# Retention layer: sums of absolute values shared between quads by adds on GpSimd, and normed images in the shared ring

## The chip, the cores and the metric

The kernel runs on one core of a Trainium2 chip. Its time is the device time of one launch in microseconds (us), the median of several runs. The core has five engines that work from queues of their own, each in order: TensorE (PE in the profile; its weight loads are PEld), VectorE (DVE), ScalarE (ACT), GpSimd (POOL) and SyncE (SP), which issues most of the transfers. Engines wait for one another through semaphores. Matrix products are written to a small memory of their own, PSUM, which VectorE and ScalarE read and GpSimd does not in this kernel.

## The reference

Four layers are applied one after the other to 8 images of 32 x 32 tokens with 256 channels, each as `x = x + layer(group_norm(x))`. The change touches the first layer alone, a retention layer with 8 heads of 32 channels. Cut to what matters:

```python
q, k, v = xf @ Wq.T, xf @ Wk.T * 32 ** -0.5, xf @ Wv.T     # per head: 1024 tokens x 32
qr, kr = theta_shift(q, sin, cos), theta_shift(k, sin, cos)  # x*cos + rotated(x)*sin
qk = einsum('bhqd,bhkd->bhqk', qr, kr) * mask                # 1024 x 1024 per head
den = clip(abs(qk).sum(-1), 1.0, 50000.0)
out = einsum('bhqk,bhkd->bhqd', qk / den, vr)
out = (out - mean) / sqrt(var + 1e-5) * ln_g + ln_b          # over the 32 channels of a head
out = gelu(out) @ Wo.T
```

So each score is needed twice: itself in the product with the values, and its absolute value in the sum `den` over the keys.

## The kernel before

The host hands the image over with channels in the partitions. A *quad* is the unit of the layer: `quads[n] = (b, c, h, kb)` is image `b`, four of the eight heads (`c`), half of the queries (`h`, 512 of them) and a block of 128 keys (`kb`). There are 32 quads to an image and 256 in all; what is called a position below is a quad's number within its image, 0 to 31. For quad `n` the program has

- `scores(n)`: for each of two pairs of heads (`i`) two matmuls of 32 channels into a tile `s` of two PSUM banks, and one product on VectorE (L681) with the mask, which gives `e[n, i]`, 128 keys x two heads x 512 queries;
- `absolute(n, i)`: ScalarE's absolute value `ea[n, i]` of that (L685), in a ring of four buffers;
- `sums(n)`: four matmuls with a column of ones (L693), one head each, side by side in the four groups of columns of the array, which add up `ea` over the keys in the PSUM tile `sm`; the eight quads of one `(b, c, h)` accumulate, and after the last VectorE clamps the sum to `dn` (L701);
- `nums(n)`: four matmuls with the values, also side by side (L720), which accumulate in `num`; after the eighth ScalarE copies it to `nm` (L728).

The loop in the last lines of `layer0` emits for each `n` scores and first absolute value, sums of quad `n - 2`, products with the values of quad `n - 1`, the second absolute value, and then `fill.emit(n)`: the units of other work that `fill.add(at, unit)` put down for this quad, ordered by `at`. Units that take matmuls are the projections `project` (each half of the queries or keys of four heads, then a shuffle on VectorE, a copy on ScalarE and the rotation on GpSimd, L560 to L567), the values `values`, the variance `var` and the output `output`. They take the place of a pair in the ring of three two-bank PSUM tiles that the scores use (`pair`, three buffers). `tail` prepares the norm over a head's channels: Square of `dn` on ScalarE, square of `nm` on GpSimd (L578) and their sum (L579), and then mean by matmul, logarithm and exponential, the product on VectorE (L591) and Gelu.

For the next image, group statistics (`gn.stats`, `gn.mean`, `gn.root`) and `normed(b + 1)` (two GpSimd operations, L236) are spread as units too. The normed image `xn` has one buffer of its own, and the images `x` share a ring of three buffers (`K.big`) with first tiles of the next layer; an image is loaded two images ahead, at position 16.

The order of TensorE, VectorE and ScalarE is the order in which the program is written (`manual_schedule`); the order on GpSimd and SyncE is set by the scheduler. Every engine works its queue in order, so a unit that waits holds up all that is written after it on its engine.

Of the kernel before, what the change touches and what calls it, by code (L numbers as in the profile page):

```python
# [436 lines left out]

class Fillers:
# [22 lines left out]
def layer0(tc, K, src, dst, n_img, a, first):  # L461
    nc = tc.nc
    with tc.tile_pool(name="l0c", bufs=1) as cp, tc.tile_pool(
# [51 lines left out]
        xn, v, qk, hT, nm, dn, turned = ({} for _ in range(7))  # L515
# [5 lines left out]
        def normed(b):  # L521
            gn.shift(b)
            xn[b] = wk.tile([P, 2, L], F32, name="xn")
            for c in range(2):
                gn.apply(nc.gpsimd, b, c, xn[b][:, c, :], x[b][:, c, :])
# [16 lines left out]
        def project(b, s, c, h):  # L542
# [13 lines left out]
            if h == 0:  # L556
                return
            d = wk.tile([P, L], F32, name=f"qk{s}{c}")
            qk[b, s, c] = d
            nc.gpsimd.tensor_mul(v3(sh), v3(sh), hankel(63))  # L560
            nc.gpsimd.tensor_mul(v3(xc), v3(xc), hankel(0))
            if s == 1:
                nc.gpsimd.tensor_add(d, xc, sh)
            else:
                nc.gpsimd.tensor_add(xc, xc, sh)
                o = 126 + 32 * c
                nc.gpsimd.tensor_mul(  # L567
                    v3(d), v3(xc), rot[:, o : o + 32].unsqueeze(2).to_broadcast([P, 32, 32])
                )


        def tail(b, c):
            m, d = nm.pop((b, c)), dn.pop((b, c))
            if c == 0:
                hT[b] = wk.tile([P, 2, L], F32, name="hT")
            nc.scalar.activation(d, d, AF.Square, scale=math.sqrt(1e-5))
            sq = wk.tile([P, L], F32, name="sq")
            nc.gpsimd.tensor_mul(sq, flat(m), flat(m))  # L578
            nc.gpsimd.tensor_add(sq, sq, flat(d))  # L579
# [17 lines left out]
            return var, norm  # L597
# [16 lines left out]
        def prepare(b):  # L614

            n = 32 * b
            for i in range(4):
                fill.add(
                    n + (0, 1, 3, 4)[i],
                    lambda s=1 - i // 2, h=i % 2: project(b, s, 1, h),  # L620
                )
            if b == 0 and n_img > 1:
                x[1] = load(1)
                measure(1, 6)
            if b + 2 < n_img:
                def ahead():
                    x[b + 2] = load(b + 2)

                fill.add(n + 16, ahead)
                measure(b + 2, n + 23)  # L630
            if b + 1 < n_img:
                fill.add(n + 15, lambda: normed(b + 1))
                for i in range(4):
                    fill.add(
                        n + (17, 18, 20, 21)[i],
                        lambda s=1 - i // 2, h=i % 2: project(b + 1, s, 0, h),
                    )
                    fill.add(n + 23 + i, lambda u=i: values(b + 1, u))

        def measure(b, at):  # L640
            for i in range(4):
                fill.add(at + i, lambda i=i: gn.stats(b, image_parts(x[b]), i))
            fill.add(at + 5, lambda: gn.mean(b))
            fill.add(at + 7, lambda: gn.root(b))

        def follow(nx):
            n = 32 * n_img
            for i, u in enumerate(nx.early()):
                fill.add(2 + i if i else 0, u)
            fill.add(n - 46, nx.load)  # L650
            for i in range(4):
                fill.add(n - 38 + i, lambda i=i: nx.stats(i))
            fill.add(n - 33, nx.mean)
            fill.add(n - 31, nx.root)
            for c in range(2):
                fill.add(n - 27 + c, lambda c=c: nx.norm(c))
            fill.add(n - 12, nx.weights)
# [9 lines left out]

        def scores(n):
            b, c, h, kb = quads[n]
            o = (28 - 4 * kb) * 32 + HALF * h  # L670
            for i in range(2):
# [11 lines left out]
        def absolute(n, i):  # L683
            ea[n, i] = wk.tile([P, 2, HALF], F32, name="ea", bufs=4)
            nc.scalar.activation(ea[n, i], e[n, i], AF.Abs)  # L685

        def sums(n):
            b, c, h, kb = quads[n]
            if kb == 0:
                acc["sm"] = pp.tile([P, HALF], F32, tag="sm", name="sm")  # L690
            for j in range(4):
                g = slice(32 * j, 32 * j + 32)
                nc.tensor.matmul(  # L693
                    acc["sm"][g, :], ones, ea[n, j // 2][:, j % 2, :],
                    start=kb == 0, stop=kb == 7,
                )
            del ea[n, 0], ea[n, 1]
            if kb == 7:
# [5 lines left out]
                if h == 1:  # L704
                    var, norm = tail(b, c)
                    fill.add(n + 7, var)
                    for h in range(2):
                        fill.add(n + 9 + h, lambda h=h: norm(h))
                    if c == 1:
                        for i in range(4):  # L710
                            fill.add(n + 12 + i, lambda i=i: output(b, i // 2, i % 2))

        def nums(n):
# [11 lines left out]
            if kb == 7:  # L725
                if h == 0:
                    nm[b, c] = wk.tile([P, 2, HALF], F32, name="nm", bufs=2)
                nc.scalar.copy(nm[b, c][:, h], acc["num"])  # L728

        engines = {mybir.EngineType.PE, mybir.EngineType.DVE, mybir.EngineType.Activation}  # L730
        with tc.manual_schedule(engines=engines):
# [3 lines left out]
            normed(0)  # L735
            for s in (1, 0):
                for h in range(2):
                    project(0, s, 0, h)
            for u in range(4):
# [4 lines left out]
            for n in range(N + 2):  # L744
# [5 lines left out]
                if n >= 2:  # L750
                    sums(n - 2)
# [1611 lines left out]
```

## Time and profile before

| what | value |
|---|---|
| median of 3 runs | 3330.99 us (3329.07 to 3332.86) |
| the profiled execution's own time | 3334.75 us |
| its span | 3333.0 us |
| busy in the span: TensorE, VectorE, ScalarE, GpSimd | 96%, 66%, 68%, 45% |
| mean granted clock of TensorE | 0.976 |
| first layer | about 0 to 1090 us of the span |
| period of one image within it (issue of output to issue of output) | 130.36 us |

A line of the timeline or of a group reads: engine, line of the kernel, operation, tile written <- tiles read, and shapes; `x8` counts instructions, and a float32 matmul is two of them. Idle time before an instruction is followed by `<-` and what ended it. Position of a quad and the loop's `n` are not in the profile; they are counted from the groups of scores (L675).

### The profile page before, as it was taken

Reading aid. Unit: us, or ns where it says so; the run is one execution under the profiler, and the core shown is the slowest. Engines: PE = TensorE matmul, PEld = TensorE weight load, DVE = VectorE, ACT = ScalarE, POOL = GpSimd, SP = SyncE. Lnnn points to the kernel's source line nnn. Section 1 sums busy time; section 2 is a strip of 40 time slices with the busy share of each in tenths; the row PEclk is TensorE's granted clock in tenths of the full one; section 3 lists DMA queues with packets and bytes.
Section 4 is the critical chain, followed back from the end, with each engine's and each line's share of the span. In section 5 each row is a group of like instructions: output and inputs, shape, how many; then the busy total and the mean of one; then the engine's idle time right before and its main releaser. Section 6 shows DMA issues by size and latency. Waiting matters only on the chain. (4 is left out here: it accounts for less than half of the span.)

```text
span 3333.0 us, 77642 instructions
## 1 busy us (share of the span) xinstructions
PE 3203.6 (96%) x30792; PEld 1649.6 (49%) x30792; DVE 2185.0 (66%) x5570; ACT 2277.6 (68%) x5066; POOL 1491.7 (45%) x1073
## 2 busy tenths in 40 slices
PE   7999999999998999899999999999998999999997
PEld 3323323233232444667677766666664555555554
DVE  4776776777676667565555655666665667777775
ACT  3666666666676457755556547767676779888885
POOL 4233223323431011245444445344335658888777
PEclk9999999999999999999999999999998889999999
DMA  3000000000000666777787731111111001101001
GB/s 141 14 26 1 26 26 1 26 7 20 26 1 32 221 235 238 234 202 191 193 216 200 187 115 58 53 65 40 50 52 36 14 14 38 35 30 36 27 27 61
DMA packets 139183, 268.00 MB, mean 80 GB/s; under 512 B 9218, under 2 KB 77700, under 8 KB 130500
## 3 DMA queue, kind: packets, MB, share of 16 engines
q1 hardware_dynamic: 132436, 242.67, 24.3%
q10 hardware_dynamic: 6384, 20.37, 1.8%
q8 instruction: 243, 3.98, 0.5%
q14 instruction: 120, 0.98, 0.1%
HBM read 177.81 MB, written 85.20 MB: 79 GB/s over the span
## 5 line engine op out<-in xcount | busy, mean ns | idle before, releaser
L681 DVE TENSOR_TENSOR e<-s,ret 128x1024 f32<-128x1024 f32 x512 | 602.9, 1219 | 180.4 <-PE s L675 176.4
L685 ACT ACTIVATE ea<-e 128x1024 f32<-128x1024 f32 x512 | 535.1, 1055 | 267.8 <-DVE e L681 233.9
L675 PE MATMUL s<-qk,qk 32*128 32x512 f32 x2048 | 300.4, 640 | 2.4 <-POOL qk L567 1.7
L1564 POOL TENSOR_TENSOR e<-e,su 128x616 f32<-128x616 f32 (+2 forms) x128 | 157.3, 1229 | 269.8 <-DVE su L1563 240.2
L693 PE MATMUL sm<-ea,ones 128*32 128x512 f32 x2048 | 273.0, 604 | 2.0 <-DVE dn L701 2.0
L720 PE MATMUL num<-e,v 128*32 128x512 f32 x2048 | 266.6, 592 | 0.0
L1711 DVE COPY pts<-pt 112x512 f32<-112x512 f32 x256 | 175.9, 687 | 133.4 <-PE pt L1706 131.7
L2076 ACT ACTIVATE e<-win,disc 128x196 f32<-128x196 f32 x512 | 239.7, 544 | 0.3
L843 PE MATMUL up_ps<-x,wup 128*128 128x512 f32 x512 | 230.7, 605 | 3.2 <-POOL x L236 3.2
L1696 POOL TENSOR_TENSOR e<-e,su 128x784 f32<-128x784 f32 x128 | 191.3, 1495 | 82.7 <-DVE su L1695 53.9
L1688 ACT ACTIVATE e<-e,mx 128x196 f32<-128x196 f32 x512 | 228.0, 454 | 0.0
L2083 POOL TENSOR_TENSOR e<-e,win 128x784 f32<-128x784 f32 x128 | 201.7, 1576 | 37.8 <-issue 31.6
L1559 ACT ACTIVATE e<-e,mx 128x154 f32<-128x154 f32 (+2 forms) x512 | 212.3, 426 | 0.0
L1059 ACT ACTIVATE d<-d,cols 128x128 f32<-128x128 f32 x512 | 163.8, 392 | 67.9 <-POOL d L1050 67.8
L870 DVE SCALAR_TENSOR_TENSOR cv<-xm,par,cv 128x512 f32<-128x512 f32 x192 | 144.7, 754 | 85.5 <-ACT cv L865 80.9
L2015 PE MATMUL qkv_ps<-xq,w 128*128 128x512 f32 x384 | 191.4, 625 | 1.2 <-ACT fac L2110 1.2
L1255 POOL TENSOR_TENSOR decayed<-state,rb 128x520 f32<-128x520 f32 x48 | 50.8, 1058 | 304.7 <-PE sc L1188 112.5
L1796 PE MATMUL qkv_ps<-x,w 128*128 128x512 f32 x384 | 182.7, 613 | 1.6 <-POOL x L236 1.6
L1706 PEld LDWEIGHTS pt<-idg,e 128*112 128x112 f32 x1024 | 120.3, 139 | 120.5 <-issue 90.6
L675 PEld LDWEIGHTS s<-qk,qk 32*128 32x128 f32 x2048 | 85.3, 183 | 184.2 <-issue 120.4
L1706 PE MATMUL pt<-idg,e 128*112 128x128 f32 x1024 | 164.7, 287 | 8.4 <-DVE oT L1730 3.1
L1678 DVE CUSTOM_DVE_ANT_0 e<-s,e 128x196 f32<-128x196 f32 x512 | 153.7, 357 | 8.0 <-PE s L1665 4.2
(244 smaller groups left out, 6775.6 us busy)
## 6 DMA issues: line engine op xcount, KB each, us to landing
d<-l1rows SPq DMA_DIRECT2D x64, 512.0 KB
x<-x SPq DMA_DIRECT2D x25, 1024.0 KB
l1xm<-xm SPq DMA_DIRECT2D x16, 1024.0 KB
l1sz<-sz SPq DMA_DIRECT2D x16, 1024.0 KB
xv<-l1xm SPq DMA_DIRECT2D x32, 512.0 KB
l1xa<-xa SPq DMA_DIRECT2D x16, 1024.0 KB
xa<-l1xa SPq DMA_DIRECT2D x16, 1024.0 KB
rb<-l1rows SPq DMA_DIRECT2D x32, 512.0 KB
```

The costliest lines, as they stand in the source:

```text
L675: nc.tensor.matmul(s[:, j % 2], qk[b, 1, c][g, kb * P : (kb + 1) * P], qk[b, 0, c][g, h * HALF : (h + 1) * HALF], start=True, stop=True,)
L681: nc.vector.tensor_mul(e[n, i], s, m)
L685: nc.scalar.activation(ea[n, i], e[n, i], AF.Abs)
L693: nc.tensor.matmul(acc["sm"][g, :], ones, ea[n, j // 2][:, j % 2, :], start=kb == 0, stop=kb == 7,)
L720: nc.tensor.matmul(acc["num"][g, :], v[b][:, kb, vc], e[n, j // 2][:, j % 2, :], start=kb == 0, stop=kb == 7,)
L843: nc.tensor.matmul(ps, wup[:, kc, m * P : (m + 1) * P], seg(s)[:, kc], start=kc == 0, stop=kc == 1,)
L1559: self.nc.scalar.activation(p[:, j], p[:, j], AF.Exp, scale=-1.0, bias=mx[:, j : j + 1], accum_out=su[:, j : j + 1],)
L1688: self.nc.scalar.activation(e[:, j], e[:, j], AF.Exp, scale=-1.0, bias=mx[:, j : j + 1], accum_out=self.su[:, j : j + 1],)
L1706: self.nc.tensor.transpose(ps[: self.PART, at : at + P], self.tile(n)[:, 2 * i + j, k * self.PART : (k + 1) * self.PART], self.K.ident,)
L2015: nc.tensor.matmul(ps, w[:, kc, o : o + P], xq[b][:, kc, h * HALF : (h + 1) * HALF], start=kc == 0, stop=kc == 1,)
L2076: nc.scalar.activation(e[:, j], win[:, 0], AF.Tanh, scale=disc[b][:, i, 8 + h : 9 + h], bias=disc[b][:, i, h : h + 1],)
L2083: nc.gpsimd.tensor_add(e, e, win[:, 1].unsqueeze(1).to_broadcast([P, 4, NWIN]))
```

## The change

Absolute values of two consecutive quads are added before they are summed, for two of the four heads in turn. In quads 0 and 1 of each group of four the order of the head pairs is `(0, 1)`, in quads 2 and 3 it is `(1, 0)`; on every odd quad GpSimd adds the quad before to the first pair in place. Four quads then have six tiles `ea` instead of eight, and three sets of sums take them, at the fourth quad of the group and at the first and second of the next; the third quad of a group has no sums. The ring of `ea` has six buffers.

With it go: GpSimd's order is now the written one too; the rotation is split in units of one operation (`rotate`), one per quad; the square of `nm` becomes a unit of its own (`squared`), and Square and sum become the unit `total`; the normed image comes from the shared ring (`K.big`), so that an image is loaded one image ahead at position 9, has its statistics at 12 and 13, mean and root at 15 and 16 and its two norm operations at 18 and 19; positions of projections and values move; and `follow` places the first pieces of the next layer accordingly.

```diff
-        def normed(b):
-            gn.shift(b)
-            xn[b] = wk.tile([P, 2, L], F32, name="xn")
-            for c in range(2):
-                gn.apply(nc.gpsimd, b, c, xn[b][:, c, :], x[b][:, c, :])
+        def normed(b, c):
+            if c == 0:
+                gn.shift(b)
+                xn[b] = K.big("xn")
+            gn.apply(nc.gpsimd, b, c, xn[b][:, c, :], x[b][:, c, :])
...
+        def rotate(b, s, c, i):
+
+            sh, xc = turned[0], turned[1]
+            if i == 0:
+                qk[b, s, c] = wk.tile([P, L], F32, name=f"qk{s}{c}")
+                nc.gpsimd.tensor_mul(v3(sh), v3(sh), hankel(63))
+            elif i == 1:
+                nc.gpsimd.tensor_mul(v3(xc), v3(xc), hankel(0))
+            elif i == 2:
+                nc.gpsimd.tensor_add(qk[b, s, c] if s else xc, xc, sh)
+            else:
+                o = 126 + 32 * c
+                nc.gpsimd.tensor_mul(
+                    v3(qk[b, s, c]), v3(xc),
+                    rot[:, o : o + 32].unsqueeze(2).to_broadcast([P, 32, 32]),
+                )
+
+        def squared(b, c):
+            sqs[b, c] = wk.tile([P, L], F32, name="sq")
+            m = flat(nm[b, c])
+            nc.gpsimd.tensor_mul(sqs[b, c], m, m)
...
-            nc.scalar.activation(d, d, AF.Square, scale=math.sqrt(1e-5))
-            sq = wk.tile([P, L], F32, name="sq")
-            nc.gpsimd.tensor_mul(sq, flat(m), flat(m))
-            nc.gpsimd.tensor_add(sq, sq, flat(d))
+            def total():
+                nc.scalar.activation(d, d, AF.Square, scale=math.sqrt(1e-5))
+                nc.gpsimd.tensor_add(sq, sq, flat(d))
...
+            def heads(b, c, at):
+                for k, s in enumerate((1, 0)):
+                    for h in range(2):
+                        fill.add(at[2 * k] + h, lambda s=s, h=h: project(b, s, c, h))
+                    for i in range(4 - s):
+                        fill.add(at[2 * k + 1] + i, lambda s=s, i=i: rotate(b, s, c, i))
+
+            heads(b, 1, (n, n + 3, n + 7, n + 9))
+            if b + 1 < n_img:
+                def ahead():
+                    x[b + 1] = load(b + 1)
+
+                fill.add(n + 9, ahead)
+                for i in range(4):
+                    fill.add(
+                        n + 12 + i // 2,
+                        lambda i=i: gn.stats(b + 1, image_parts(x[b + 1]), i),
+                    )
+                fill.add(n + 15, lambda: gn.mean(b + 1))
+                fill.add(n + 16, lambda: gn.root(b + 1))
+                for c in range(2):
+                    fill.add(n + 18 + c, lambda c=c: normed(b + 1, c))
+                heads(b + 1, 0, (n + 20, n + 22, n + 25, n + 27))
+                for i in range(4):
+                    fill.add(n + (22, 24, 28, 30)[i], lambda u=i: values(b + 1, u))
...
+        def order(n):
+
+            return (0, 1) if n % 4 < 2 else (1, 0)
+
         def scores(n):
...
-            for i in range(2):
+            for i in order(n):
...
-        def absolute(n, i):
-            ea[n, i] = wk.tile([P, 2, HALF], F32, name="ea", bufs=4)
+        def absolute(n, k):
+
+
+            i = order(n)[k]
+            ea[n, i] = wk.tile([P, 2, HALF], F32, name="ea", bufs=6)
             nc.scalar.activation(ea[n, i], e[n, i], AF.Abs)
-
-        def sums(n):
+            if n % 2 and k == 0:
+                nc.gpsimd.tensor_add(ea[n, i], ea[n, i], ea.pop((n - 1, i)))
+
+        def sums(n, k):
+
             b, c, h, kb = quads[n]
-            if kb == 0:
+            if kb == 0 and k == 0:
                 acc["sm"] = pp.tile([P, HALF], F32, tag="sm", name="sm")
+            two = [ea.pop((n + (1, 2, 3)[k], 0)), ea.pop((n + (0, 1, 3)[k], 1))]
             for j in range(4):
                 g = slice(32 * j, 32 * j + 32)
                 nc.tensor.matmul(
-                    acc["sm"][g, :], ones, ea[n, j // 2][:, j % 2, :],
-                    start=kb == 0, stop=kb == 7,
-                )
...
+                    acc["sm"][g, :], ones, two[j // 2][:, j % 2, :],
+                    start=kb == 0 and k == 0, stop=kb == 4 and k == 2,
+                )
...
-                    var, norm = tail(b, c)
-                    fill.add(n + 7, var)
+                    total, var, norm = tail(b, c)
+                    fill.add(n + 6, total)
+                    fill.add(n + 10, var)
                     for h in range(2):
-                        fill.add(n + 9 + h, lambda h=h: norm(h))
+                        fill.add(n + 12 + h, lambda h=h: norm(h))
...
-        with tc.manual_schedule(engines=engines):
+        E = mybir.EngineType
+        with tc.manual_schedule(engines={E.PE, E.Activation, E.DVE, E.Pool}):
...
-                if n >= 2:
-                    sums(n - 2)
+                if n % 4 == 3:
+                    sums(n - 3, 0)
+                elif n % 4 < 2 and n > 1:
+                    sums(n // 4 * 4 - 4, n % 4 + 1)
```

In positions of the image: projections at 0, 1, 7, 8 (second four heads) and 20, 21, 25, 26 (the next image); rotations at 3 to 5, 9 to 12, 22 to 24 and 27 to 30; values at 22, 24, 28 and 30; `squared` at 0 and 16, `total` at 2 and 18, `var` at 6 and 22, `norm` at 8, 9, 24 and 25, outputs at 11 to 14 (of the image before); adds on GpSimd at every odd position; no sums at 2, 6, 10 and so on.

## The prediction

> **What bounds the kernel now.** I read the page first: TensorE is busy for 96% of the span, in every slice. The change touches only the first layer, some 0 to 1090 us; the instruction order of the two built programs is the same on every engine from the next layer's first instruction on. So the second view is busy time by stretch, one image long:
>
> ```profile
> 351.44:481.80 130.36, 129.67 (x864) 39.74 (x860) 92.23 (x105) 88.23 (x92) 42.41 (x21) 1.00 0.05 17
> ```
>
> Columns: length, then TensorE, weight loads, VectorE, ScalarE, GpSimd, granted clock, DMA. An image takes 130.36 us (two outputs later: 130.35), and TensorE works in 129.67 of them; GpSimd in 42. The third view, the timeline, shows one quad without filler and the start of the next one's filler:
>
> ```profile
> 310.96 1.14 PE L675 MATMUL s<-qk,qk 32*128 32x512 f32 x8
> 312.04 1.07 PE L693 MATMUL sm<-ea,ones 128*32 128x512 f32 x8
> 312.21 2.36 DVE L681 TENSOR_TENSOR e<-s,ret 128x1024 f32<-128x1024 f32 x2 [0.57 <-PE s L675]
> 312.92 1.04 PE L720 MATMUL num<-e,v 128*32 128x512 f32 x8
> 313.53 2.19 ACT L685 ACTIVATE ea<-e 128x1024 f32<-128x1024 f32 x2 [0.74 <-DVE e L681]
> 313.89 1.98 PE L550 MATMUL qk_ps<-xn,w 128*128 128x512 f32 x4
> 315.80 0.71 PE L675 MATMUL s<-qk,qk 32*128 32x512 f32 x4
> ```
>
> From start to start: scores 1.07, sums 0.88, products with the values 0.97, together 2.92 us; a filler (projection, values, output, variance) adds 1.92. VectorE starts 1.25 after the scores and needs 2.36; ScalarE starts 1.32 after VectorE and needs 2.19 for both halves. 32 quads and 18 fillers make 128 of the 130.36 us: TensorE's queue is the bound and nearly without a hole.
>
> Fourth, groups by line (busy, mean ns) for what moves on GpSimd:
>
> ```profile
> L579 POOL TENSOR_TENSOR sq<-sq,dn 128x1024 f32<-128x1024 f32 x12 | 28.7, 2390 | 39.0 <-ACT dn L576 39.0
> L565 POOL TENSOR_TENSOR xc<-xc,sh 128x1024 f32<-128x1024 f32 x12 | 28.6, 2379 | 0.9
> ...
> L578 POOL TENSOR_TENSOR sq<-nm 128x1024 f32<-128x1024 f32 x12 | 22.7, 1892 | 43.2 <-ACT nm L728 43.2
> L567 POOL TENSOR_TENSOR qk<-xc,rot 128x1024 f32<-128x1024 f32 x11 | 21.1, 1917 | 0.9
> ...
> L236 POOL TENSOR_SCALAR xn<-x,gn 128x1024 f32<-128x1024 f32 x12 | 14.2, 1195 | 171.7 <-issue 165.7 <-DVE gn L230 6.0
> ```
>
> **What is removed.** 64 of 256 sets of sums, 256 matmuls of four concurrent heads: 64 x 0.88 = 56.3 us off TensorE's queue. Three small stalls of before go as well: the projection at position 4 of an image waits for the buffers of the rotation (315.80 to 321.21 is 5.41 where 4.84 is usual; 7 such waits, 3.3 us), which the spread rotations end: 3.5. The sums behind the clamp `dn` (a quad of 3.18 instead of 2.92): 8 x 0.26 = 2. The second of two stalls round the group statistics, shown below: 7 x 0.41 = 2.9. Together 64.7 us.
>
> **What is added.** 128 sums of absolute values on GpSimd. No such add is in the trace; between 1.89 (L578, one source) and 2.40 (the longest of L579) I take 2.38, for L565 is the same in-place form. 16 x 2.38 = 38 us an image make GpSimd 42 + 38 = 80 of 130: room on average, but its queue is now in hand-written order and TensorE waits for single adds. I went through an image quad by quad. Most adds come out ahead of their sums; these places do not (positions are quads within an image, times from the start of the scores there):
>
> 1. *Norm of the next image.* GpSimd's order round position 18 is first normed half, sum of squares `total`, add of 19, second normed half, and the projection at 20 needs both halves. VectorE starts at 1.37 (0.12 late, the clamp of 17 lies before), ScalarE's pair ends 3.51 later at 4.88, Square (1.06) 5.94, `total` from 6.08 (0.14 hand-over) to 8.47, add 10.85, second half 12.05. TensorE is at its second half of the projection after 2.04 (no sums at 18) + 3.48 + 2.92 + 0.96 = 9.40. Stall 2.7, 7 images.
> 2. *`total` before the add of position 3.* Likewise from position 2: 4.76, 5.82, 5.96, 8.35, add 10.73; TensorE wants these sums (at 5) at 2.04 + 3.36 + 2.92 + 1.07 = 9.39. Stall 1.4, 7 images.
> 3. *Last rotation.* From position 29: add 3.77 to 6.15, then 2.37 and 1.92 of rotation to 10.5; the next image's scores are due at 2.92 + 3.96 + 2.92 = 9.80. Stall 0.77, 7 images.
> 4. *Ring of score tiles.* With three pairs of banks, the second pair of the next scores needs the first product of this quad. The trace shows this wait where a quad's tile is taken by the statistics:
>
> ```profile
> 417.54 1.04 PE L720 MATMUL num<-e,v 128*32 128x512 f32 x8
> 418.51 0.38 PE L200 MATMUL gn_ps<-gn_mv,idg 128*128 128x2 f32 x2
> 418.82 1.54 PE L675 MATMUL s<-qk,qk 32*128 32x512 f32 x8
> 420.29 1.07 PE L693 MATMUL sm<-ea,ones 128*32 128x512 f32 x8
> ```
>
> Scores to sums is 1.47 instead of 1.07. A quad with neither sums nor filler lasts 2.04, while the first product is ready at 1.25 + 1.18 = 2.43: 0.44 at 2, 0.56 at 18, and 0.8 at 10, where VectorE is late by the norm products of 8 and 9. 1.8 x 8 images = 14.4 (bounds 0 and 0.8 at each).
> 5. *Projection at 7* waits 0.2 for a tile that Ln frees: 1.4 in all. *End of the layer:* the last sums follow an add that ends 6.2 after their quad's scores; before, they began 4.53 after (1060.94 to 1065.47): 1.6.
>
> **The clock.** A stall of 2.7 costs more than itself. Timeline, and stretches of 1 us (second number TensorE's busy time, third from the end the granted clock):
>
> ```profile
> 39.99 1.14 PE L675 MATMUL s<-qk,qk 32*128 32x512 f32 x8 [1.70 <-POOL qk L567]
> ```
> ```profile
> 39.00:40.00 1.00, 0.01 (x1) 0.01 (x1) 0.00 (x0) 0.00 (x0) 0.94 (x1) 1.00 0.00 0
> 40.00:41.00 1.00, 1.00 (x8) 0.31 (x8) 0.00 (x0) 0.00 (x0) 0.00 (x0) 1.00 0.00 0
> 42.00:43.00 1.00, 1.00 (x2) 0.43 (x2) 1.00 (x2) 0.57 (x1) 0.00 (x0) 0.50 0.00 0
> 43.00:44.00 1.00, 1.00 (x2) 0.00 (x0) 0.53 (x1) 0.93 (x2) 0.00 (x0) 0.50 0.00 0
> 45.00:46.00 1.00, 1.00 (x12) 0.16 (x8) 0.57 (x2) 0.52 (x1) 0.00 (x0) 1.00 0.00 0
> ```
>
> After 1.70 us without work the clock is 0.50 for about 3.4 us; gaps of 1.71 (1110.37) and 1.58 (2036.25) do the same, one of 1.9 (1985.6) does not, and gaps of 1.00 (1566.87) do not. So stall 1 costs another 3.4 x 0.5 = 1.7, seven times. In stall 2 the first two heads' sums run during the wait, which leaves some 0.5 idle: nothing.
> The Trainium skill, "TensorE: Matmul & The Clock Gate", section "HAM oscillation — how this bites in real kernels", would allow gaps up to about 3.4 us. By that rule the seven drops would not come and the time would be near 3318. The 1.70-us gap above speaks against it, and I go by the row.
>
> **Costed at nothing.** The load of the next image now issues after the projection at 8; its predecessor issued at 95.87 had stopped moving data at 101.1, and the statistics read it 13 us later, at 12. In SyncE's queue it stands ahead of the outputs at 12 and 14, so its wait holds nothing up. Outputs that must leave before the normed image takes their slot are issued by 14, and move for some 2 us; the norm is at 18. Both become a wait on VectorE or GpSimd, and so on TensorE, only if the transfer grew by 7 us. VectorE (92 us an image) and ScalarE (88) keep their work and stay below TensorE's 123. The products on VectorE show 2.35 to 2.36 a pair whether GpSimd works (312.21) or not (416.83).
>
> **Sum.** Against: 7 x (2.7 + 1.4 + 0.77 + 1.7) = 46.0, ring 14.4, places in 5 together 3.0: 63.4. For: 64.7. Net 1.3 us less. The profiled execution took 3334.75, 3.8 above the median of 3330.99; applied to the median, 3330: no change beyond 0.2% (6.7 us), which is about what a measurement here can tell.
>
> **Rivals.**
> - *Slower: the clock also halves in the stalls of 1.4 and 0.77.* For it: three of four gaps of 1.6 to 1.9 did so, and the limit is not seen. Against: the gap of 1.00 and the half-filled stall 2. Price 14 x 1.7 = 24: 3354; from four such drops on (6.8) it is slower. 0.21.
> - *Slower: GpSimd's operations stretch.* Eight of them stand in stalls 1 to 3, so 0.1 us each is 8 x 7 x 0.1 = 5.6 us; from 0.13 on it is slower, at 0.2 it is 3341. Against: 2.34 for the sum with the other engines idle (1068.77), 2.39 among them. 0.15.
> - *Faster: no drop of the clock, or adds of 1.89.* 11.9 less, 3318; or 0.49 less in each of three chains, 7 x 1.5 = 10: 3320. For it: the gap at 1985.6. 0.23.
> - *Faster: no add is late*, because what I queue behind each other overlaps: 46 less, 3284. For it: 80 of 130. Against: one queue, in order. 0.05.
> - That the change does not do what it says is out: the built program has 256 fewer matmuls and 128 more GpSimd adds.
>
> **Chances and range.** No change 0.36; faster 0.28; slower 0.36. From 3311 (the first faster case with 7 us of error) to 3354, which leaves out the last faster case and what lies above the clock's price. The likeliest case alone: 3323 to 3337.
>
> **What the profile after will show.** TensorE in the first layer down by 256 matmuls; an image near 130 us still, with GpSimd near 80 busy; TensorE's waits for GpSimd on `xn`, `ea` and `qk`, about 2.7, 1.4 and 0.8 each, seven times; clock below 1.00 once an image, behind the first. I am wrong if the wait for `xn` is under 1.5 or over 4, if other waits exceed 10 us in sum, or if VectorE's product grows from 1.22.

## The result, and the profile after

The changed kernel takes 3367.21 us (median of 4 runs, 3359.74 to 3371.68) against 3331.93 us of the kernel before beside it (4 runs, 3329.07 to 3334.19). The ratio is 1.0106, with a 95% interval of 1.0087 to 1.0124: 35 us slower, where no change was forecast. The profiled execution took 3371.68 us, its span is 3369.9 us, 36.9 more than before's.

The first layer gives most of it: the next layer's first matmul stands at 1119.9 us instead of 1089.6, 30.3 later. The rest comes after it. Busy time by stretch of the changed kernel, cut at that matmul (columns as in the prediction: length, TensorE, weight loads, VectorE, ScalarE, GpSimd, granted clock, DMA), and one image from output to output:

```profile
1119.90:3369.90 2250.00, 2154.54 (x23869) 1322.87 (x23867) 1441.29 (x4700) 1568.78 (x4329) 1142.16 (x874) 0.97 0.36 106
```
```profile
495.45:628.80 133.35, 128.79 (x800) 38.81 (x796) 95.55 (x105) 87.62 (x92) 80.72 (x37) 0.97 0.05 17
```

After the layer the same 23869 TensorE instructions take 2250.0 us; before they took 2243.4. In the trace's record of the granted clock, the clock is at one half for 151.1 us of this stretch against 141.1 before, which is some 5 of the 6.6 us. No instruction there has moved, so the later layers' gaps probably fall elsewhere against the clock's steps (below). In the first layer the clock is at one half for 78.5 us against 20.5: 58 us more, some 29 us lost. An image of that layer takes 133.35 us instead of 130.36, though it has 64 TensorE instructions fewer. GpSimd works 80.7 us of it, as forecast, but the clock is 0.97.

Where TensorE waits, between 100 and 1090 us of the changed kernel (line that waits, who is waited for, total in us, times, longest):

```profile
PE qk_ps L552 <- POOL xn L236: 15.6, 7, 2.2
PE s L687 <- DVE e L693: 14.3, 10, 1.9
PE s L687 <- POOL qk L571: 3.3, 7, 0.5
```

The first and the third are stalls 1 and 3 of the prediction. The second is in no step of it as a gap. Seven of its ten, 1.70 us each, stand between the two pairs of scores of position 11, in every image but the first. Timeline of the changed kernel around positions 9 to 11, VectorE, GpSimd and TensorE:

```profile
478.42 1.14 PE L687 MATMUL s<-qk,qk 32*128 32x512 f32 x8
479.21 2.36 POOL L702 TENSOR_TENSOR ea<-ea 128x1024 f32<-128x1024 f32 x1 [6.04 <-DVE e L693]
479.68 2.44 DVE L601 TENSOR_TENSOR sq<-nm,sq 128x512 f32<-128x512 f32 x1
480.49 1.13 PE L687 MATMUL s<-qk,qk 32*128 32x512 f32 x4
481.53 2.64 POOL L564 TENSOR_TENSOR sh<-sh,rot 128x1024 f32<-128x1024 f32 x1
482.04 4.60 DVE L693 TENSOR_TENSOR e<-s,ret 128x1024 f32<-128x1024 f32 x4
483.31 1.13 PE L687 MATMUL s<-qk,qk 32*128 32x512 f32 x4 [1.70 <-DVE e L693]
485.76 1.95 PE L739 MATMUL num<-e,v 128*32 128x512 f32 x8
```

The norm product of 512 columns (L601) takes 2.44 us here. It begins 0.47 us after GpSimd's add (L702) and ends 0.55 us after the add's end. So VectorE is late with the masked products of position 10, the ring of score tiles has nothing free, and TensorE stands for 1.70 us; the add that saves TensorE time makes VectorE lose it, just where position 10 has neither sums nor filler. (The first image has no norm at 8 and 9, and no such gap.) Then the clock falls, as the stretches of 1 us show (third number from the end), and the matmuls with the values take 1.95 instead of 1.04:

```profile
482.00:483.00 1.00, 0.00 (x0) 0.00 (x0) 1.00 (x2) 0.80 (x1) 1.00 (x1) 1.00 0.00 0
485.00:486.00 1.00, 1.00 (x12) 0.33 (x8) 1.00 (x2) 1.00 (x2) 1.00 (x1) 0.50 0.00 0
486.00:487.00 1.00, 1.00 (x9) 0.00 (x0) 0.65 (x1) 1.00 (x2) 0.35 (x1) 0.50 0.00 0
```

Groups by line of VectorE, 100 to 850 us, first of before, then of the changed kernel (busy, mean ns):

```profile
L681 DVE TENSOR_TENSOR e<-s,ret 128x1024 f32<-128x1024 f32 x368 | 433.4, 1219 | 126.7 <-PE s L675 124.4 <-ACT xc L555 0.8 <-ACT ea L685 0.7
L591 DVE TENSOR_TENSOR sq<-nm,sq 128x512 f32<-128x512 f32 x22 | 14.7, 668 | 0.0
```
```profile
L693 DVE TENSOR_TENSOR e<-s,ret 128x1024 f32<-128x1024 f32 x360 | 422.9, 1218 | 123.2 <-PE s L687 122.6 <-issue 0.4
L601 DVE TENSOR_TENSOR sq<-nm,sq 128x512 f32<-128x512 f32 x22 | 36.5, 1659 | 0.0
```

The norm product has gone from 668 to 1659 ns. The masked product, which the prediction had looked at, is unchanged at 1218 (before 1219). The first reads two tiles of SBUF, the second one of SBUF and one of PSUM.

The product at 9 is not the only one that is late. Of an image's four, those at 24 and 25 meet GpSimd too, and only the one at 8 keeps its 0.68 us:

```profile
544.41 2.21 POOL L566 TENSOR_TENSOR xc<-xc,rot 128x1024 f32<-128x1024 f32 x1
544.60 2.56 DVE L601 TENSOR_TENSOR sq<-nm,sq 128x512 f32<-128x512 f32 x1
549.57 2.36 POOL L702 TENSOR_TENSOR ea<-ea 128x1024 f32<-128x1024 f32 x1 [0.16 <-ACT ea L700]
551.61 0.88 DVE L601 TENSOR_TENSOR sq<-nm,sq 128x512 f32<-128x512 f32 x1
```

In the first layer 23 of the 32 products meet a GpSimd operation. They begin between 0.18 and 2.04 us into it and take 0.87 to 2.57 us, but every one of them ends 0.54 to 0.56 us after GpSimd's operation does. At 24 and 25 TensorE hardly stalls, for values and projections stand there to fill it. In the last image they are missing, and the product at 25 makes the same gap at position 27, the longest of the ten:

```profile
1073.25 2.36 POOL L702 TENSOR_TENSOR ea<-ea 128x1024 f32<-128x1024 f32 x1
1073.73 2.43 DVE L601 TENSOR_TENSOR sq<-nm,sq 128x512 f32<-128x512 f32 x1
1077.35 1.13 PE L687 MATMUL s<-qk,qk 32*128 32x512 f32 x4 [1.87 <-DVE e L693]
```

### The profile page after: what moved, and what is told of

It reads as the page before. It is cut to its first block, busy times and chain, and to the rows that moved or that the text cites. A ratio compares the mean times of both kernels' runs of the same rounds, so it can differ in the third digit from the quotient of the medians.

```text
span 3369.9 us, 76338 instructions
## 1 busy us (share of the span) xinstructions
PE 3205.8 (95%) x30280; PEld 1647.3 (49%) x30280; DVE 2211.8 (66%) x5570; ACT 2272.5 (67%) x5066; POOL 1797.2 (53%) x1201
## 4 chain that ended last, share of the span: by engine, by line
PE 68%; ACT 13%; POOL 8%; DVE 5%; issue 5%; DMA 1%; ACTq 0%; POOLq 0%; SPq 0%; DVEq 0%
PE s L687 7%; PE qkv_ps L1822 5%; PE up_ps L869 5%; PE num L739 4%; PE sm L712 4%; PE qkv_ps L2041 4%; PE qk_ps L552 4%; PE pt L1604 3%; PE pt L1732 2%; PE dn_ps L1349 2%; PE fac_ps L2143 2%; ACT e L2102 2%; DVE e L693 2%; PE o_ps L613 2%; POOL ea L702 2%
## 5 line engine op out<-in xcount | busy, mean ns | idle before, releaser
L693 DVE TENSOR_TENSOR e<-s,ret 128x1024 f32<-128x1024 f32 x512 | 601.2, 1218 | 183.3 <-PE s L687 182.6
L702 POOL TENSOR_TENSOR ea<-ea 128x1024 f32<-128x1024 f32 x128 | 303.4, 2371 | 357.4 <-ACT ea L700 304.9
L687 PE MATMUL s<-qk,qk 32*128 32x512 f32 x2048 | 324.3, 655 | 20.2 <-DVE e L693 14.3
L739 PE MATMUL num<-e,v 128*32 128x512 f32 x2048 | 281.1, 609 | 0.0
L712 PE MATMUL sm<-ea,ones 128*32 128x512 f32 x1536 | 222.0, 628 | 0.6 <-POOL ea L702 0.3
L687 PEld LDWEIGHTS s<-qk,qk 32*128 32x128 f32 x2048 | 92.5, 186 | 218.9 <-issue 77.2
```

Of the source, the lines that this page charges most:

```text
L687: nc.tensor.matmul(s[:, j % 2], qk[b, 1, c][g, kb * P : (kb + 1) * P], qk[b, 0, c][g, h * HALF : (h + 1) * HALF], start=True, stop=True,)
L693: nc.vector.tensor_mul(e[n, i], s, m)
L702: nc.gpsimd.tensor_add(ea[n, i], ea[n, i], ea.pop((n - 1, i)))
L712: nc.tensor.matmul(acc["sm"][g, :], ones, two[j // 2][:, j % 2, :], start=kb == 0 and k == 0, stop=kb == 4 and k == 2,)
L739: nc.tensor.matmul(acc["num"][g, :], v[b][:, kb, vc], e[n, j // 2][:, j % 2, :], start=kb == 0, stop=kb == 7,)
```

## The experiments

The theory after this reading: GpSimd's operation on two tiles of SBUF shuts a VectorE product of two tiles of SBUF out until it ends; that makes the gap at position 11, and a gap of this length lowers the clock. The other losses are those of the prediction. The rivals: the engines merely share the way to the memory; or VectorE is late there by its own load; or the new positions and rings cost the time, without the adds.

**One norm product earlier.** The second product of the norm goes to position 8, where GpSimd adds nothing.

```diff
-                        fill.add(n + 12 + h, lambda h=h: norm(h))
+                        fill.add(n + 12 + (h if c == 0 else 0), lambda h=h: norm(h))
```

> The second norm product of the second four heads goes from position 9 to position 8, next to the first. In the changed kernel VectorE's norm product (two operands in SBUF) takes 2.44 us at position 9, where a GpSimd add runs, instead of 0.67; position 10 has no sums and no filler, and positions 10 and 11 together take 4.5 us too long per image. Theory (VectorE's product is shut out while GpSimd's add runs): the two products take about 0.7 each at 8, the gap of 1.70 us on TensorE at position 11 and the clock drop after it are gone, 3 to 3.7 us less an image, 24 to 30 in all: 3337 to 3343. Rival (it is the place without sums and filler with its ring of score tiles, whatever the product takes): VectorE has the same work before the scores' product of 10, so the time stays within 6 us of 3367.

Measured: 3342.33 us, ratio to before 1.0037 [1.0026, 1.0048], so 25 us less than the changed kernel and inside the range of the theory, though partly by luck: positions 10 and 11 take 8.92 us instead of 11.37, 7 x 2.45 = 17 us, and the other 8.0 us lie at positions 20 and 21, where the clock fell less often, which the edit did not aim at. In its timeline both products take 1.27 together, and the 1.70-us gap is gone:

```profile
466.33 1.27 DVE L601 TENSOR_TENSOR sq<-nm,sq 128x512 f32<-128x512 f32 x2
...
471.24 2.37 POOL L702 TENSOR_TENSOR ea<-ea 128x1024 f32<-128x1024 f32 x1 [7.96 <-ACT ea L700]
...
473.67 1.06 PE L712 MATMUL sm<-ea,ones 128*32 128x512 f32 x8 [0.89 <-POOL ea L702]
```

What is late next is the add of position 9: two products in a row delay VectorE, and the sums wait 0.89 us for GpSimd. Moving one product of 0.7 us takes the gap away; that it collides where it stood is shown, though not yet why. The gap at position 27 of the last image, where this edit moves nothing, is still there.

**The add at position 9 in two halves.**

```diff
-                nc.gpsimd.tensor_add(ea[n, i], ea[n, i], ea.pop((n - 1, i)))
+                prev = ea.pop((n - 1, i))
+                if n % 32 == 9:
+                    for j in range(2):
+                        nc.gpsimd.tensor_add(ea[n, i][:, j], ea[n, i][:, j], prev[:, j])
+                else:
+                    nc.gpsimd.tensor_add(ea[n, i], ea[n, i], prev)
```

> The GpSimd add at position 9 alone is made as two operations of one head each, same bytes. Theory (shut out for the length of one GpSimd operation): the norm product at position 9 waits for one half at most, so it takes 0.7 to 1.9 us instead of 2.44, the gap on TensorE falls below 1.2 us and the clock drop after it mostly goes: 10 to 24 us less, 3343 to 3357. Rival (the two engines share bandwidth, each slows the other in proportion): the product still overlaps the same bytes, stays at 2.2 to 2.5, and the time stays at 3367 within 6 us, or grows by the fixed cost of eight more operations.

Measured: 3340.23 us, ratio 1.0029 [1.0016, 1.0042], 3 us below the range of the theory and 27 below the 3367 of shared bandwidth; position 11 gives 7 x 2.73 = 19 us of it, and some 3 us are clocks at position 20 again. The product meets only the first half, ends 0.55 us after it and takes 1.35 us; the gap falls to 0.62 us and lowers no clock:

```profile
471.56 2.96 POOL L705 TENSOR_TENSOR ea<-ea 128x512 f32<-128x512 f32 x2 [6.02 <-DVE e L693]
472.04 1.35 DVE L601 TENSOR_TENSOR sq<-nm,sq 128x512 f32<-128x512 f32 x1
474.58 1.13 PE L687 MATMUL s<-qk,qk 32*128 32x512 f32 x4 [0.62 <-DVE e L693]
```

Here VectorE reads and GpSimd writes as much as before, and in the same place. The length of GpSimd's single instruction decides, which speaks for an exclusive hold and against sharing.

**Normed images and `total` out of each other's way on GpSimd.**

```diff
-            heads(b, 1, (n, n + 3, n + 7, n + 9))
+            heads(b, 1, (n, n + 4, n + 7, n + 9))
...
-                    fill.add(n + 18 + c, lambda c=c: normed(b + 1, c))
+                    fill.add(n + 17 + c, lambda c=c: normed(b + 1, c))
...
-                    fill.add(n + 6, total)
+                    fill.add(n + 7, total)
```

> The two halves of the next image's norm go to positions 17 and 18, ahead of the sum of squares, which goes to 3 and 19 behind the add there; the first rotation goes from 3 to 4. Theory (GpSimd's queue order makes TensorE wait 2.8 us at 20 with a clock drop of 1.7 behind it, 1.1 at 5): these waits go, 7 x (2.8 + 1.3 + 0.5 to 1.1) = 32 to 36 us less: 3331 to 3335, with the gap at position 11 still there. Rival (GpSimd is short of time as a whole, 80 of 133 us with the waits for inputs): the wait moves to another add or to the rotation, and the time falls by less than 15 us.

Measured: 3319.09 us, ratio 0.9975 [0.9963, 0.9988]: 48 us less than the changed kernel, 12 below the lower end of what the theory expected, and faster than before. The waits for `xn` are gone, and position 5 takes 2.92 us instead of 4.02. The collision at position 9 is untouched, 2.44 us, and so is the gap, but here the clock stays up behind it:

```profile
460.29 2.44 DVE L601 TENSOR_TENSOR sq<-nm,sq 128x512 f32<-128x512 f32 x1
```
```profile
463.92 1.13 PE L687 MATMUL s<-qk,qk 32*128 32x512 f32 x4 [1.70 <-DVE e L693]
464.97 1.06 PE L712 MATMUL sm<-ea,ones 128*32 128x512 f32 x8
465.86 1.04 PE L739 MATMUL num<-e,v 128*32 128x512 f32 x8
```

Position 11 takes 2.83 + 4.82 = 7.65 us against 9.30 in the changed kernel; 4.84 would be usual. So the gap itself costs 2.8 us and the clock 1.65. Of the seven gaps after 100 us three lowered the clock here, and all seven did in the changed kernel. So most of the first layer's 44.9 us less (1075.0 instead of 1119.9) is accounted for: 28.6 at positions 20 and 21, 7 x 1.10 at position 5, and 5.1 at position 11 for lowered clocks that the edit did not aim at (four fewer, but one of the three left lasts two steps), 41.4 in all.

**No adds, in the changed schedule.** Four sets of sums for four quads as before; all positions, rings and the written order of GpSimd as in the changed kernel, but for the positions that count from the last sums.

```diff
-            if n % 2 and k == 0:
-                nc.gpsimd.tensor_add(ea[n, i], ea[n, i], ea.pop((n - 1, i)))
...
-            two = [ea.pop((n + (1, 2, 3)[k], 0)), ea.pop((n + (0, 1, 3)[k], 1))]
+            two = [ea.pop((n, 0)), ea.pop((n, 1))]
...
-                    fill.add(n + 6, total)
+                    fill.add(n + 3, total)
```

> The changed schedule with no adds on GpSimd and four sets of sums for four quads, as before; all else as in the changed kernel. Theory (the adds on GpSimd cause the waits, by its queue and by shutting VectorE out): TensorE works without holes but for the norm product against the rotation at 9: 3325 to 3338, within 7 us of before. Rival (the moved units, one image loaded ahead and the image ring cost the time): TensorE's 56 us come back on top of the 35, 3390 to 3420.

Measured: 3338.72 us, ratio 1.0021 [1.0007, 1.0035], 0.7 us above the range of the theory and over 50 below that of the rival. No clock is lowered between 100 and 1060 us, and there is no wait for `xn`: the adds bring the large losses, not the rings or the load. But the schedule alone is not faster than before either, though it ends two of the three small stalls. The third, behind the clamp `dn`, stays (3.5 us in 15 waits, before 2.0 in 9), and one is new: the norm product collides here too, with the rotation that now stands at position 9.

```profile
467.53 2.22 POOL L566 TENSOR_TENSOR xc<-xc,rot 128x1024 f32<-128x1024 f32 x1
468.27 2.03 DVE L601 TENSOR_TENSOR sq<-nm,sq 128x512 f32<-128x512 f32 x1
470.26 2.36 PE L687 MATMUL s<-qk,qk 32*128 32x512 f32 x8
```

With sums at position 10, TensorE's queue is long enough that this costs 1.2 us an image (6.02 instead of 4.84 for position 11) and no clock.

**Both moves together.** The diffs of the first and the third experiment.

> The norm product moved to position 8 and the normed images made early, together. If the two losses are separate and each edit only takes its own away, the gains add: 25 us of the first and 48 us of the second off the 3367 us, so 3294 us. If most of the second edit's 48 us was the clock (the image's period pulled away from a whole number of clock windows, 10 drops of 1.7 us fewer), the first edit has less left to save: the gap of 2.8 us an image shrinks to the 2.0 us that its own trace shows at positions 10 and 11, 0.8 x 8 = 6 us, and two drops, 3 us: 3307 to 3315 us. If the second edit had already cured the collision, nothing is left: 3319 us.

Measured: 3310.26 us, ratio 0.9938 [0.9922, 0.9955]. That is the middle case: the two gains do not add, for each edit alone had also spared lowered clocks at the other's place, the first 8.0 us at positions 20 and 21, the second 5.1 us at 11. An image takes 125.89 us at full clock, and what remains is mainly the late add of position 9, 6.5 us in 8 waits.

**VectorE's load spread around position 9.**

```diff
-            heads(b, 1, (n, n + 4, n + 7, n + 9))
+            heads(b, 1, (n, n + 4, n + 9, n + 11))
...
-                heads(b + 1, 0, (n + 20, n + 22, n + 25, n + 27))
+                heads(b + 1, 0, (n + 20, n + 22, n + 25, n + 26))
...
-                        fill.add(n + 12 + h, lambda h=h: norm(h))
+                        fill.add(n + 12 + h * (1 + c), lambda h=h: norm(h))
...
-                            fill.add(n + 15 + i, lambda i=i: output(b, i // 2, i % 2))
+                            fill.add(n + 16 + i, lambda i=i: output(b, i // 2, i % 2))
```

(against the third experiment)

> The same early normed images, and around position 9 VectorE's load spread: second projection of k and q at positions 9 and 10 instead of 7 and 8, norm products at 8 and 10, where GpSimd adds nothing, output projections one position later, and the last rotation of the next image's q one position earlier. If the collision of the norm product with GpSimd's add is what makes the gap at position 10, the product takes 0.7 us in both places, the gap of 1.7 us is gone and with it 2.8 us in each of 8 images (22 us), some 3 us of clock and about 0.5 x 7 of the last rotation: 3319 - 28 = about 3292 us, between 3286 and 3302. If VectorE is late there for its own load (denominator, product, short position), the gap only moves and the time stays at 3312 to 3322 us.

Measured: 3290.2 us, ratio 0.9884 [0.986, 0.9908]: 41 us less than before beside it and 77 less than the changed kernel, with all of its adds. An image, and TensorE's waits from 100 to 1000 us:

```profile
463.34:586.89 123.55, 123.45 (x800) 38.18 (x796) 94.70 (x105) 88.34 (x92) 80.36 (x38) 1.00 0.05 18
```
```profile
PE s L687 <- DVE e L693: 0.2, 1, 0.2
```

TensorE is busy for 123.45 of 123.55 us. Against before's 130.36 that is 6.8 us an image, of the 7.0 that eight sets of sums are worth (8 x 0.88). GpSimd does the same 80 us of work. The last image lies behind these views: there the product at 25 still meets its add (2.44 us) and makes a gap of 1.88 us at 1001.2, with a lowered clock, so that position 27 takes 6.99 us instead of 2.92. So this kernel has not lost the whole collision. The expectation of 0.7 us for both products held only for the second (0.68); the first took 1.47, since it still meets the end of an add, but the filler at positions 9 and 10 covers it.

**The collision without a saving.** One add more at position 9 in the kernel without adds, into a tile that is not read.

```diff
+            if n % 32 == 9 and k == 0:
+                idle = wk.tile([P, 2, HALF], mybir.dt.bfloat16, name="idle")
+                nc.gpsimd.tensor_add(idle, ea[n, i], ea[n, i])
```

> The kernel without adds (3338.7 us), with one add of a quad's absolute values into a tile that nobody reads, at position 9 of each image, issued where the changed kernel issues its add there. Nothing waits for it. If the two engines shut each other out, the second norm product at position 9 goes from 0.7 us to 2.2 to 2.5 us all the same, VectorE is 1.7 us late, and the following positions, all with sums and so with 2.92 us of TensorE work, take back 0.5 us each of it: 0.3 to 1.2 us lost an image, 3341 to 3350 us. If the product in the changed kernel was slow for another reason (its own wait, its place in the queue), it stays at 0.7 us and the time at 3336 to 3340 us.

Measured: 3336.53 us, ratio 1.0019 [1.0007, 1.0032], no slower than without that add. The product takes 1.97 us:

```profile
468.35 1.89 POOL L703 TENSOR_TENSOR idle<-ea 128x1024 bf16<-128x1024 f32 x1 [14.97 <-DVE e L693]
```
```profile
468.82 1.97 DVE L601 TENSOR_TENSOR sq<-nm,sq 128x512 f32<-128x512 f32 x1
```

This told the theories less apart than meant. The expectation took the product for 0.7 us without the add, and it was 2.03 already, behind the rotation. The add only took the rotation's place as the blocker. What it shows is that the product ends 0.55 us after whichever GpSimd operation it meets, a third one here.

**More work, to shift the gaps.** The third experiment suggested that the lowered clocks depend on where a gap falls. Two kernels repeat a variance matmul of each image, once or twice:

```diff
-                for h, hs in halves():
+                for h, hs in list(halves()) + list(halves())[:1] * (1 if c == 0 else 0):
```

> The changed kernel, with one variance matmul of each image's first two heads done twice (a repeat that changes no result): 0.94 us of TensorE work more in each of 8 images, 7.5 us, at position 22, where nothing waits. In the changed kernel both gaps of an image (1.70 us at position 10, 2.23 us at position 20) are followed by a lowered clock in nearly every image, and the image takes 133.35 us, 39.07 of the 3.41-us steps on which the clock changes. If it is the place of a gap against these steps that decides, an image of another length loses that lock: with both drops it would be 39.34 steps long, with one 38.86, so that the gaps wander, and 5 to 9 drops are left of the 13 before the layer's end: 3367 + 7.5 - (4 to 8) x 1.65 = 3362 to 3368 us. If a gap of this length always lowers the clock, 13 drops stay and it is 3367 + 7.5 = 3374 to 3375 us.

> The same with the matmul done three times: 1.88 us more an image, 15 us in all. With both drops an image would be 39.62 steps long, with one 39.13. If the place against the steps decides, 5 to 9 drops are left: 3367 + 15 - (4 to 8) x 1.65 = 3369 to 3375 us. If every such gap lowers the clock: 3382 us.

Measured: 3376.7 us (3369.68 to 3379.18, ratio 1.0128 [1.0103, 1.0152]) and 3384.57 us (3370.14 to 3389.97, ratio 1.0147 [1.0109, 1.0186]). The expectation that the gaps would wander failed: of 14 gaps, 13 and 12 still lowered the clock, and the times are 9.5 and 17.4 us up for 7.5 and 15 us of work. But these traces help to see when a gap lowers the clock, below.

**The second factor of the norm product in PSUM.** Nothing is moved but ScalarE's Exp, which now stands with the first product.

```diff
-                nc.scalar.activation(sq, sq, AF.Exp, scale=-0.5)
+
+            inv = {}

             def norm(h):
+                if h == 0:
+                    inv[0] = pair("inv")
+                    nc.scalar.activation(flat(inv[0]), sq, AF.Exp, scale=-0.5)
                 hs = slice(h * HALF, (h + 1) * HALF)
-                nc.vector.tensor_mul(sq[:, hs], m[:, h], sq[:, hs])
+                nc.vector.tensor_mul(sq[:, hs], m[:, h], inv[0][:, h])
```

> The changed kernel, with the second factor of the norm product in PSUM instead of SBUF: ScalarE's Exp is issued at the place of the first norm product and writes into a pair of banks of the ring of score tiles, and the two products read it there. Positions, adds and everything else stay. If what shuts the product out is a path to SBUF that GpSimd's two-operand add holds, and that a product with one operand in PSUM doesn't need, the product at position 9 takes 0.7 us while GpSimd adds, VectorE is 1.7 us less late there, and the gap at position 10 shrinks to below 0.6 us, with no lowered clock behind it: 20 to 30 us less than 3367 us, unless the pair that the ring lends takes more; its price, in the wait for score tiles at positions 8 to 10, is between 0 and 2 us an image, so 3337 to 3360 us. If any VectorE product of two tensors is shut out while GpSimd adds, it stays at 1.7 to 2.6 us, and the time at 3367 us or above.

Measured: 3360.81 us, ratio 1.0083 [1.0058, 1.0108]. Timeline and group (100 to 850 us):

```profile
482.22 2.37 POOL L706 TENSOR_TENSOR ea<-ea 128x1024 f32<-128x1024 f32 x1 [8.84 <-DVE e L697]
```
```profile
482.70 0.68 DVE L605 TENSOR_TENSOR sq<-nm,inv 128x512 f32<-128x512 f32 x1
```
```profile
L605 DVE TENSOR_TENSOR sq<-nm,inv 128x512 f32<-128x512 f32 x22 | 15.0, 681 | 25.3 <-ACT inv L603 25.3
```

The product stands in the same place, inside the same add, and takes 0.68 us; the longest of all 32 is 0.69. GpSimd's next operation, 2.64 in the changed kernel, is back at 2.21. The gap at position 11 is gone, with its lowered clock. So it is the product with both operands in SBUF that is shut out. The time gains only 6 us, just outside the range: VectorE now waits for Exp (25.3 us in this stretch), and the pair that the ring lends is paid for by TensorE, with 6.1 us of waits at the scores and a later start of several positions.

## Why the prediction was wrong, point by point

| step of the prediction | forecast, us | measured, us | from |
|---|---|---|---|
| 1, norm of the next image, stall and clock | 7 x 4.4 = 30.8 | 28.6 in sum, mostly 4.08 | positions 20 and 21 take 7.61 + 6.15 instead of 2 x 4.84 |
| 2, `total` before the add of 3 | 7 x 1.4 = 9.8 | 7 x 1.10 = 7.7 | position 5 takes 4.02 instead of 2.92 |
| 3, last rotation | 7 x 0.77 = 5.4 | 7 x 0.55 = 3.9 | the last position takes 3.47 instead of 2.92 |
| 4, ring at 2 and 18 | 8 x 1.0 = 8.0 | 8 x 0.90 = 7.2 | the position after takes 3.37 instead of 2.92 |
| 4, ring at 10 | 8 x 0.8 = 6.4 | 7 x 4.46 + 4.5 = 35.7 | position 11 takes 9.30 instead of 4.84, position 27 of the last image 7.46 instead of 2.92 |

**The step that failed** is "0.8 at 10, where VectorE is late by the norm products of 8 and 9", with its bounds "0 and 0.8 at each". The mechanism was right: the ring, behind a late VectorE. The size was not. The products were evidently taken as 0.67 us each, as before has them, and the one at 9 takes 2.44. Of the 4.46 us, 2.8 is the gap and its restart and 1.65 the lowered clock, which this step had not counted at all. The number of times is eight as forecast, but by luck: the first image has no norm at 8 and 9, and the eighth gap is the one at position 27 of the last image, which no step names. The difference, 35.7 - 6.4 = 29.3 us, is nearly the whole error: the forecast was 1.3 us less in the first layer, this makes it 28.0 more, and 30.3 was measured. It is shown by three runs that each take the collision away by other means (another place, a shorter instruction, another memory), and each time the gap goes or shrinks with it.

**Why the bound was too narrow.** The upper end of 0.8 came from VectorE working at its old speed. The prediction looked whether GpSimd slows VectorE, and found "2.35 to 2.36 a pair whether GpSimd works (312.21) or not (416.83)". That row is of the masked product, with one operand in PSUM, and it holds after the change as well. The norm product has two in SBUF, and in before it never met GpSimd (668 ns, all alike), so no row of before had its price. But the places were known: the walk through an image had both the product at 9 and the add at 9 in it, on two engines, and did not set them against each other. The Trainium skill, "SBUF — State Buffer", section "SBUF: two separate sides", says that VectorE and GpSimd share a pair of ports as an exclusive lock: of a VectorE operation with two inputs in SBUF and a GpSimd operation that reads SBUF, the one that starts first has the pair for its whole instruction, and the other is blocked. The runs agree, with 2.44 us against 0.68 when one input is in PSUM, and with 23 products that all end some 0.55 us after GpSimd. The list of what would prove the prediction wrong named "VectorE's product", but only the one of 1.22. Another sign on it did come: the waits other than for `xn` were to stay within 10 us in sum, and were 14.3 + 3.3 = 17.6. That VectorE would keep its work of 92 us an image did not hold either; it is 95.55.

**What held.** Stalls 1 to 3 and the ring at 2 and 18 came within 0.4 us each, from rows of before alone. The adds took 2371 ns where 2380 was assumed. The lowered clock behind stall 1 came in six of seven images. The choice there of the row with a gap of 1.70 us over the page's rule, which allows gaps up to some 3.4 us, was right. In the rival of stretching GpSimd operations the sign was right, but what stretched and cost time was VectorE's product.

**What the gains came to.** The sums and the three small stalls did go. An image in the middle of the layer takes 133.35 us against 130.36, 2.99 more. The table's rows cost 4.08 + 1.10 + 0.55 + 0.90 + 4.46 us of it and the wait at position 7 costs 0.17; eight sets of sums (7.04) and the stalls (0.57 + 0.26 + 0.41) are saved, which makes 2.98. What the prediction lacks besides lies in the first image. It takes 130.94 us against 128.01, where steps 1, 3 and 4 and its saved sums would make it 3.1 shorter. Of these 6.0 us, 3.4 are a third lowered clock, at 85.37 us, and TensorE idles 0.68 and 1.72 us before matmuls on the next layer's `prep` tiles, which GpSimd has not finished; the kernel without adds has neither wait. Together this leaves some 5 of the 30.3 us untraced. In the kernel without adds the written order of GpSimd puts a rotation on the norm product, at 1.2 us an image.

**What a rival had right.** "80 of 130", no add late, 3284 us, was given 0.05 as a forecast for this kernel, and rightly little. As a bound it was good: with the collisions and queues moved apart, the same work runs at 3290.

## What to carry to other kernels

When work moves to GpSimd, list the VectorE instructions that read two tiles of SBUF, put their places beside GpSimd's, and price each meeting at what is left of the GpSimd instruction, up to the whole of it, not at a share of bandwidth; an instruction with one operand in PSUM is no evidence for the others. A position that becomes shorter has no slack to hide such a delay, so look there first; to keep the change, move the two instructions apart by a position or put one operand in PSUM. Where a kernel repeats with a fixed period, a gap's cost in clock is not its length alone, and whole repetitions can pay it or be spared.

## What the runs showed of the hardware that was not expected

**The hold seems to work both ways.** In the changed kernel the rotation L564 that GpSimd begins at 481.53, while the blocked product is running, takes 2.64 us instead of 2.21; with the product's operand in PSUM it takes 2.21. The rotation L568 behind the product at 24 takes 2.72 instead of 2.37. That fits a hold in the other direction, but no run was made for it.

**At these two places, what lowers the clock is how much of a gap falls into one step.** The granted clock changes on a grid of 3.41 us (in the changed kernel it falls at 484.73, 525.69 and 617.85 us, 12.0 and 27.0 steps of 3.413 us apart). I set every gap of 1.69 to 1.70 us at position 11 and of 2.2 us before the projection at 20, after 100 us of seven traces, against that grid:

| kernel | gaps at 11, clock lowered | gaps at 20, clock lowered |
|---|---|---|
| changed | 7 of 7 | 6 of 7 |
| one product earlier | none there | 2 of 7 |
| add in halves | none there | 4 of 7 |
| normed early | 3 of 7 | none there |
| one matmul more | 6 of 7 | 7 of 7 |
| two matmuls more | 6 of 7 | 6 of 7 |
| factor in PSUM | none there | 5 of 7 |

At 11 the clock fell for every gap of which at least 1.41 us lay within one step, and for none with 1.35 or less; at 20 the limits are 1.82 and 1.76. With early normed images, for example, the gap at 970.72 lay 1.44 and 0.26 us in two steps and lowered the clock, and the one at 462.22 lay 1.35 and 0.34 and did not. That the two places differ fits with how full the rest of the step is, but this wasn't tested. Of the gaps that the prediction cites from before, those of 1.70, 1.71 and 1.58 us that lowered the clock lay whole within one step, and the one of 1.89 that did not lay 1.42 in one and 0.47 in the next. But the limits are those of two places only: of two gaps of 1.57 us in before that lie whole within one step (at 2612.4 and 2711.1) only the second lowered the clock, and one of 1.01 us (at 1948.0) lowered it as well, though the prediction took gaps of 1.00 for harmless. The Trainium skill, "TensorE: Matmul & The Clock Gate", section "Part 1: The HAM clock gate", gives a free-running window of 3413 ns, which agrees with the grid; the rule of "HAM oscillation — how this bites in real kernels", gaps up to about 3.4 us, does not.

**The phase can hold itself.** An image of the changed kernel takes 133.35 us, 39.07 steps. So a gap moves by only 0.23 us against the grid from one image to the next, and all seven fell badly; with early normed images it is 126.7 us, 37.1 steps, and four of seven were spared. When a matmul or two were added, the drops themselves lengthened the images (to 136.5 us, 40.0 steps, with two), and again nearly all fell badly. Whether a kernel settles in such a phase or slips out of it couldn't be foretold here, and stays open.
